# First batch of a fused two-layer graph attention kernel: the mask is shared between TensorE and VectorE, and the row sums leave GpSimd

## The chip, the cores and the metric

The kernel runs on one core of one Trainium2 chip. The metric is the device time of one execution in microseconds (us), the median of several runs. A core has five engines that work side by side: TensorE (PE in the profile, its weight loads PEld), VectorE (DVE), ScalarE (ACT), GpSimd (POOL), and SyncE (SP), which here only issues DMA transfers. Each engine takes its instructions strictly in the order in which the program wrote them.

## The reference, cut to what matters

There are 16 graphs (batches) of 1024 nodes with 256 features, and one 0/1 adjacency matrix per graph. Layer 0 is masked self-attention with 8 heads of width 32 followed by an MLP; layer 1 is a single-head graph attention. The change concerns the attention of layer 0:

```python
h = jnp.maximum(_layernorm(x), 0.0)
qkv = layer_norm(h, gamma1, beta1).reshape(b, n, 8, 32).transpose(0, 2, 1, 3)
scores = einsum('bhqd,bhkd->bhqk', qkv, qkv) / sqrt(32)
attn = softmax(where(adj > 0, scores, -inf), axis=-1)
out = einsum('bhqk,bhkd->bhqd', attn, qkv)
```

Queries, keys and values are the same matrix, the mask is symmetric and has the same value for all heads, and the softmax is taken without subtracting a maximum: the kernel computes exp(scale * (score + mask)), the weighted sum of values, and apart from it the row sum (the denominator).

## The kernel before, in words

One Python program writes out all 16 batches as straight-line code. Several generators ("streams") are merged by a place on a common axis, on which batch b's attention runs from b to b+1: attention (`stream_a`), the MLP and layer 1 of the batch (`stream_b`, which starts near b+0.98, so it runs beside the attention of batch b+1), the load and normalisation of the next batch (`stream_c`, `prologue`), and the load, conversion and transposition of the next masks (`stream_m`, `turn_masks`). `defer(us, f)` puts an operation off until a virtual clock has passed, and the order that comes out is the order of each engine's queue; dependencies add no engine order beyond that, since the last lines pin it. Because of these places the attention of batch 0 has no MLP beside it: only the setup of folded weights (`setup`), the second half of its own masks, and the prologue and first masks of batch 1.

The attention is cut into 32 units per batch: 2 query halves (`qh`, 512 queries) by 2 head groups (`g`, 4 heads) by 8 key tiles (`kt`, 128 keys). A unit in batch 0 is, in queue order:

- `scores`: two PSUM tiles `s` (`sc0` and `sc1`), 128 keys by 2 heads by 512 queries each, with one buffer each. TensorE first adds the mask with four matmuls of a full 128x128 fp8 identity against the mask (L874), then adds the products of keys and queries, four heads in four row groups of the array (L880, eight records because each fp32 matmul counts as two).
- ScalarE takes exp of `sc0` into `e` and later exp of `sc1` (L899).
- `weigh` of the unit before: value-weighted sums, four heads in four column quarters of the array (L912).
- `add_up` of a unit: `acc += e` for `sc0`'s half on VectorE and for `sc1`'s half on GpSimd (L931). In batches 1 to 15 the same sum is done by accumulating DMA transfers that GpSimd issues (L934).

From batch 1 on the mask isn't added by TensorE; VectorE adds it while it moves the scores from PSUM to SBUF (L896), and exp works in place. After the eight key tiles `total` multiplies `acc` by ones for the denominator (L835), `finish` transposes and divides (L852 to L859). The helper `matmul` (L567 to L570) splits a matmul into four column quarters of 32 while the flag `quarters` is set, which holds until the last attention is closed. `midp` is a pool of three 8 KB tiles (per partition) that the MLP's hidden layer and layer 1 use later and that holds the setup's `stage` at first; `ep` has five 4 KB tiles for `e`; `lp1` has six 2 KB tiles that layer 1 uses.

Of the kernel before, what the change touches and what calls it, by code (L numbers as in the profile page):

```python
# [9 lines left out]
F32 = mybir.dt.float32  # L10
# [6 lines left out]
P = 128  # L17
# [476 lines left out]
def fast_path(  # L494
# [28 lines left out]
    nc = tc.nc  # L523
    B, N, D = x.shape
    DFF = W1.shape[1]
    H, HD = 8, D // 8
    GH = 4
    NG = H // GH
    NT = N // P
    DC = D // P  # L530
    FC = DFF // P
    QW = 512
# [15 lines left out]
    midp = pool("midp", 3)  # L548
    ep = pool("ep", 5)
    accp = pool("accp", 2)  # L550
    lp1 = pool("lp1", 6)
# [6 lines left out]
    def ps_tile(shape, name, dtype=F32):  # L558
        return psm.tile(shape, dtype, tag="ps", name=name)
# [5 lines left out]
    def matmul(out, lhsT, rhs, start=True, stop=True):  # L565
        if not quarters[0]:
            nc.tensor.matmul(out, lhsT, rhs, start=start, stop=stop)  # L567
            return
        for c in range(0, P, HD):
            nc.tensor.matmul(out[c : c + HD], lhsT[:, c : c + HD], rhs, start=start, stop=stop)  # L570
# [30 lines left out]
    ones = const.tile([P, HD], F32, name="ones")  # L601
# [47 lines left out]


    def setup():
        stage = midp.tile([P, 4, DC, D], F32, tag="mid", name="stage")
        wl, wa, wT, wb = (stage[:, i] for i in range(4))
        weights_to_load.extend([(wl, W), (wa, a_12)])
        for t, src in weights_to_load:
            nc.scalar.dma_start(t, src.rearrange("(c p) n -> p c n", p=P))
        yield

        for oc in range(DC):
            pt = ps_tile([P, DC, P], f"p_wT_{oc}")  # L660
            for ic in range(DC):
                nc.tensor.transpose(pt[:, ic, :], wl[:, ic, oc * P : (oc + 1) * P], ident)
            nc.scalar.copy(wT[:, oc, :], pt.rearrange("p c q -> p (c q)"))
        clock[0] += 0.5
        yield

        def product(dst, lhs, rhs, n, name):

            for oc in range(DC):
                pp = ps_tile([P, n], f"p_{name}_{oc}")  # L670
                for kc in range(DC):
                    matmul(
                        pp,
                        lhs[:, kc, oc * P : (oc + 1) * P],
                        rhs[:, kc, :n],
                        start=(kc == 0),
                        stop=(kc == DC - 1),
                    )
                nc.scalar.copy(dst[:, oc, :], pp)

        product(wb, wa, wT, D, "wb")
        clock[0] += 1.7
        yield
        product(wm, wT, wb, D, "wm")
        product(w_a2.unsqueeze(2), wT, a2c.unsqueeze(2), 1, "w_a2")
        product(wo2[:, :, D : D + 1], wT, a1c.unsqueeze(2), 1, "w_a1")
        nc.gpsimd.memset(wo2[:, :, D + 1 : D + 2], 0.0)
        clock[0] += 2.0
        yield
# [22 lines left out]
    clock = [0.0]  # L712
    deferred = []

    def defer(us, f):
        deferred.append((clock[0] + us, len(deferred), f))

        return clock[0] + us
# [101 lines left out]
    def make_turns():  # L820
        room = 3 - open_sums[0] - bool(summed) if open_sums[0] else 100
        while turns and turns[0][0] <= room:
            n, f = turns.pop(0)
            room -= n
            f()
# [2 lines left out]

    scored, weighed, summed, totalled = [], [], [], []

    def total(b, qh, g, os, acc):

        den = ps_tile([P, QW], f"den_{b}_{g}_{qh}")
        for j in range(GH):
            nc.tensor.matmul(  # L835
                den[j * HD : (j + 1) * HD, :], ones, acc[j // 2][:, j % 2, :], start=True, stop=True
            )
        ds = tmpp.tile([P, QW], F32, tag="w2", bufs=3, name=f"ds_{b}_{g}_{qh}")
        nc.scalar.copy(ds, den)
        totalled.append((b, qh, g, ds, os))  # L840
# [20 lines left out]
    def attention(b, st):  # L861
        va, kT = st["va"], st["kT"]


        def scores(qh, g, kt):
            qs = slice(qh * QW, (qh + 1) * QW)
            sc = [
                psc.tile([P, 2, QW], F32, tag=f"sc{i}", name=f"s_{b}_{g}_{qh}_{kt}_{i}") for i in range(2)
            ]

            by_pe = b == 0
            if by_pe:
                for j in range(GH):
                    nc.tensor.matmul(  # L874
                        sc[j // 2][:, j % 2, :], ident8, st[qh][:, kt // 2, :, kt % 2], start=True, stop=False
                    )
                clock[0] += 0.9
            for j in range(GH):
                r = slice(j * HD, (j + 1) * HD)
                nc.tensor.matmul(  # L880
                    sc[j // 2][:, j % 2, :],
                    kT[r, g, kt * P : (kt + 1) * P],
                    kT[r, g, qs],
                    start=not by_pe,
                    stop=True,
                )
            mb = st[qh][:, kt // 2, :, kt % 2].unsqueeze(1).to_broadcast([P, 2, QW])
            es = []
            for i in range(2):
                if kt == 0:  # L890
                    e = accp.tile([P, 2, QW], F32, tag=f"acc{i}", name=f"acc_{b}_{g}_{qh}_{i}")
                else:
                    e = ep.tile([P, 2, QW], F32, tag="e", name=f"e_{b}_{g}_{qh}_{kt}_{i}")
                masked = sc[i]
                if not by_pe:
                    nc.vector.tensor_tensor(e, masked, mb, op=ALU.add)  # L896
                    masked = e
                es.append(e)
                weights = lambda e=e, masked=masked: nc.scalar.activation(e, masked, AF.Exp, scale=SCALE)  # L899
                if i == 0:  # L900
                    weights()
            return es, weights

        acc = {}


        def weigh(qh, g, kt, es):
            if kt == 0:
                acc[g, qh] = pso.tile([P, QW], F32, tag="o", name=f"o_{b}_{g}_{qh}")
            o = acc[g, qh]  # L910
            for j in range(GH):
                nc.tensor.matmul(  # L912
                    o[j * HD : (j + 1) * HD, :],
                    va[:, kt, (g * GH + j) * HD : (g * GH + j + 1) * HD],
                    es[j // 2][:, j % 2, :],
                    start=(kt == 0),
                    stop=(kt == NT - 1),
                )
            if kt == NT - 1:
                c = tmpp.tile([P, QW], F32, tag="w2", bufs=3, name=f"os_{b}_{g}_{qh}")  # L920
                nc.vector.tensor_copy(c, o)
                weighed.append((b, qh, g, c, sums[g, qh]))

        sums = {}


        def add_up(qh, g, kt, es):
            if b == 0:

                for e, a, engine in zip(es, sums[g, qh], (nc.vector, nc.gpsimd)):  # L930
                    engine.tensor_add(a, a, e)  # L931
                return
            for e, a in zip(es, sums[g, qh]):
                nc.gpsimd.dma_start(a, e, accum_op=ALU.add)  # L934

        units = [(qh, g, kt) for qh in range(NQH) for g in range(NG) for kt in range(NT)]
        for u in units:
            make_turns()
            es, rest_of_weights = scores(*u)
            go_on()  # L940
            rest_of_weights()
            qh, g, kt = u
            if kt == 0:
                sums[g, qh] = es
            else:
                defer(1.5, lambda u=u, es=es: add_up(*u, es))
            scored.append((weigh, (*u, es)))
            yield

    def go_on():  # L950
        was_weighed, was_summed, was_totalled = weighed[:], summed[:], totalled[:]
        for l in (weighed, summed, totalled):
            l.clear()
        if scored:
            f, args = scored.pop()
            f(*args)
        summed.extend(was_weighed)
        for args in was_summed:
            total(*args)
        for args in was_totalled:  # L960
            turns.append((2, lambda args=args: finish(*args)))
        clock[0] += 2.0
# [320 lines left out]
    def stream_a():  # L1283
        for b in range(B):
            yield from spread(attention(b, states[b]), 32, b, b + 1)
        yield from spread(close_attention(), 4, B, B + 0.05)
# [40 lines left out]
    def stream_s():  # L1327
        yield -0.3
        for i, _ in enumerate(setup()):
            yield 0.25 + 0.05 * i  # L1330
# [3 lines left out]
    while any(p is not None for p in places):  # L1334
        i = min((p, i) for i, p in enumerate(places) if p is not None)[1]
# [101 lines left out]
```

## Time and profile before

| what | value |
|---|---|
| device time, median of 3 | 3644.68 us (3642.08 to 3649.2) |
| span of the profiled execution | 3643.5 us, granted TensorE clock 0.991 |
| VectorE busy over the span | 2749.6 us (75%) |
| ScalarE busy | 1859.1 us (51%) |
| GpSimd busy | 1483.6 us (41%) |
| first mask matmul of batch 0 | at 41.47 us |
| last score matmuls of batch 0 | at 175.67 us |
| first MLP matmul | at 182.55 us |

The first batch's attention thus takes 141 us of 3643.5 us; what precedes it is the load of the first inputs and masks. Durations are of one instruction, busy times are unions of them, and "idle before" is how long the engine had stood still before the instruction, with what released it. An instruction that is stretched by another engine counts as busy for its whole length, so a long mean must be compared with the length of the same instruction elsewhere.

### The profile page before, as it was taken

How to read it: one execution, taken by the hardware profiler on the slowest of the kernel's cores; microseconds unless marked ns; L12 is line 12 of the kernel's file. 1: busy time of each engine (PE TensorE's matmuls, PEld its weight loads, DVE VectorE, ACT ScalarE, POOL GpSimd, SP SyncE). 2: the span in 40 equal slices, each digit the busy share in tenths (PEclk: the TensorE clock that was granted, in tenths of full speed). 3: DMA queues.
4: the chain of work that ended last, by engine and by line, in shares of the span. 5: the costliest groups of instructions: out<-in, count | busy, mean ns of one | idle time of the engine just before them, and what ended most of it. 6: DMA issues, size and time to landing. Idle time of an engine off the chain costs nothing.

```text
span 3643.5 us, 106813 instructions
## 1 busy us (share of the span) xinstructions
PE 3501.1 (96%) x46334; PEld 1697.8 (47%) x46334; DVE 2749.6 (75%) x5165; ACT 1859.1 (51%) x2183; POOL 1483.6 (41%) x1712
## 2 busy tenths in 40 slices
PE   5899999999999999999999999999999999999998
PEld 1244444444444444444444444444444444444477
DVE  3878878787786978768787787877868777786744
ACT  3555555555555555545555555555555555555522
POOL 4844434343443434434444343433434344343220
PEclk9999999999999999999999999999999999999999
DMA  3278988989889988888988889888988989899720
GB/s 100 67 145 169 181 164 178 191 166 177 170 177 176 175 173 169 175 157 179 189 166 168 164 174 189 170 178 164 182 168 176 169 166 181 162 180 180 148 49 13
DMA packets 278978, 585.19 MB, mean 161 GB/s; under 512 B 94562, under 2 KB 129764, under 8 KB 278500
## 3 DMA queue, kind: packets, MB, share of 16 engines
q0 software_dynamic: 120960, 440.46, 65.9%
q1 hardware_dynamic: 152580, 134.27, 14.3%
q8 instruction: 366, 6.00, 0.7%
q10 hardware_dynamic: 4960, 3.55, 0.4%
q14 instruction: 112, 0.92, 0.1%
HBM read 104.21 MB, written 16.78 MB: 33 GB/s over the span
## 4 chain that ended last, share of the span: by engine, by line
PE 75%; DMA 10%; DVE 7%; issue 4%; ACT 2%; POOL 2%; DVEq 0%; POOLq 0%; SPq 0%; ACTq 0%
PE s L880 13%; PE o L912 11%; PE pa L570 10%; PE ph L570 10%; PE lg L570 9%; DMA acc<-e 9%; PE po L570 7%; PE pf L570 2%; DVE e L896 2%; PE pg L570 2%; PE puT L570 2%; PE den L835 1%; ACT e L899 1%; DVE e L1153 1%; PE pa L567 1%
## 5 line engine op out<-in xcount | busy, mean ns | idle before, releaser
L899 ACT ACTIVATE e<-e 128x1024 f32<-128x1024 f32 x840 | 884.8, 1057 | 1018.8 <-DVE e L896 763.5
L934 POOL DMA_DIRECT2D acc<-e x840 | 740.3, 893 | 1553.4 <-DMA acc<-e 680.3
L896 DVE TENSOR_TENSOR e<-s,mk 128x1024 f32<-128x1024 f32 x840 | 988.5, 1217 | 170.3 <-PE s L880 96.1
L880 PE MATMUL s<-kT 32*128 32x512 f32 x4096 | 617.1, 649 | 3.9 <-DVE e L896 3.9
L912 PE MATMUL o<-e,va 128*32 128x512 f32 x3584 | 487.3, 614 | 1.6 <-ACT e L899 1.6
L570 PE MATMUL ph<-yT,w 128*32 128x256 f32 x7808 | 450.2, 381 | 4.7 <-DVE yT L1033 4.7
L570 PE MATMUL pa<-gw,e 128*32 128x258 f32 x7552 | 449.1, 382 | 0.0
L570 PE MATMUL lg<-fT,uT 128*32 128x256 f32 x7680 | 445.1, 379 | 0.0
L570 PE MATMUL po<-w,hid 128*32 128x256 f32 x7680 | 441.8, 381 | 0.0
L570 PEld LDWEIGHTS ph<-yT,w 128*32 128x32 f32 x7808 | 254.9, 110 | 220.1 <-issue 54.0
L570 PEld LDWEIGHTS po<-w,hid 128*32 128x32 f32 x7680 | 251.4, 111 | 211.6 <-issue 66.2
L570 PEld LDWEIGHTS pa<-gw,e 128*32 128x32 f32 x7552 | 251.3, 111 | 210.8 <-issue 63.1
L570 PEld LDWEIGHTS lg<-fT,uT 128*32 128x32 f32 x7680 | 250.3, 110 | 209.0 <-issue 39.6
L1153 DVE SCALAR_TENSOR_TENSOR e<-lg,gw,mk 128x256 f32<-128x256 f32 x512 | 223.0, 476 | 65.5 <-PE lg L570 57.2
L1056 DVE TENSOR_TENSOR hid<-ph,b1c 128x512 f32<-128x512 f32 x256 | 175.1, 687 | 125.6 <-PE ph L570 112.2
L1159 ACT ACTIVATE e<-e,shift 128x512 f32<-128x512 f32 x256 | 183.0, 716 | 139.6 <-DVE e L1158 114.8
L880 PEld LDWEIGHTS s<-kT 32*128 32x128 f32 x4096 | 170.8, 185 | 174.7 <-issue 106.8
L912 PEld LDWEIGHTS o<-e,va 128*32 128x32 f32 x3584 | 71.7, 108 | 348.3 <-issue 202.7
L1158 DVE SCALAR_TENSOR_TENSOR e<-e 128x512 f32<-128x512 f32 x256 | 198.6, 776 | 8.8
L899 ACT ACTIVATE acc<-acc 128x1024 f32<-128x1024 f32 x120 | 126.9, 1058 | 143.5 <-DVE acc L896 139.1
L769 POOL TENSOR_TENSOR nrm<-nrm,g 128x256 f32<-128x256 f32 x128 | 118.9, 929 | 85.0 <-DVE nrm L706 85.0
L896 DVE TENSOR_TENSOR acc<-s,mk 128x1024 f32<-128x1024 f32 x120 | 141.1, 1217 | 14.3 <-PE s L880 14.3
(136 smaller groups left out, 3939.9 us busy)
## 6 DMA issues: line engine op xcount, KB each, us to landing
acc<-e POOLq DMA_DIRECT2D x840, 512.0 KB, 5.9
adj<-in_adj_dram SPq DMA_DIRECT2D x256, 256.0 KB, 5.0
h<-in_x_dram SPq DMA_DIRECT2D x64, 256.0 KB, 7.1
xb<-in_x_dram SPq DMA_DIRECT2D x128, 128.0 KB, 5.3
out_dram<-z SPq DMA_DIRECT2D x128, 128.0 KB, 3.1
w<-in_L_gnn_W_dram ACTq DMA_DIRECT2D x2, 1024.0 KB, 10.3
mk<-mq SPq DMA_TRANSPOSE x128, 6.2
wo<-in_L_gnn_W_dram ACTq DMA_DIRECT2D x2, 256.0 KB, 3.9
```

What stands on the lines that cost most here:

```text
L567: nc.tensor.matmul(out, lhsT, rhs, start=start, stop=stop)
L570: nc.tensor.matmul(out[c : c + HD], lhsT[:, c : c + HD], rhs, start=start, stop=stop)
L769: nc.gpsimd.tensor_mul(nrm, nrm, g1)
L880: nc.tensor.matmul(sc[j // 2][:, j % 2, :], kT[r, g, kt * P : (kt + 1) * P], kT[r, g, qs], start=not by_pe, stop=True,)
L896: nc.vector.tensor_tensor(e, masked, mb, op=ALU.add)
L899: weights = lambda e=e, masked=masked: nc.scalar.activation(e, masked, AF.Exp, scale=SCALE)
L912: nc.tensor.matmul(o[j * HD : (j + 1) * HD, :], va[:, kt, (g * GH + j) * HD : (g * GH + j + 1) * HD], es[j // 2][:, j % 2, :], start=(kt = ...
L934: nc.gpsimd.dma_start(a, e, accum_op=ALU.add)
L1056: nc.vector.tensor_tensor(hid[:, f0 : f0 + 2, :], ph, b1c[:, f0 : f0 + 2].unsqueeze(2).to_broadcast([P, 2, CW]), op=ALU.add,)
L1153: nc.vector.scalar_tensor_tensor(e[:, j, :], lg[:, j, :], gw[:, kt, D : D + 1], st[c // 2][:, kt // 2, qs, kt % 2], op0=ALU.add, op1=ALU.add,)
L1158: nc.vector.scalar_tensor_tensor(e, e, ALPHA, e, op0=ALU.mult, op1=ALU.max)
L1159: ready = defer(2.5, lambda: nc.scalar.activation(e, e, AF.Exp, bias=shift))
```

## The change

Only batch 0 is touched, apart from the place of the setup's staging tiles.

- Mask: TensorE adds it only for heads 0 and 1 (`sc0`), through `matmul`, so in column quarters. For heads 2 and 3 VectorE adds it as in the later batches, `e = sc1 + mask`, and exp works in place. The virtual clock counts 0.45 us for it in place of 0.9.
- Row sums: GpSimd adds nothing. Even key tiles go into `acc` by accumulating DMA as in the later batches. Odd key tiles go into tiles `odd` of the pool `midp`; VectorE adds the former odd tile to the present one, half by half, deferred by 1.0 and 3.5 us after `weigh`.
- `total` multiplies both `acc` and the last `odd` by ones and sums in PSUM.
- `stage` moves from one 8 KB tile of `midp` to four 2 KB tiles of `lp1`, which leaves all three `midp` tiles for `odd`.

The purpose is to take half of the mask matmuls from TensorE and all of the 128x1024 additions from GpSimd.

```diff
--- before.py
+++ after.py
@@ -649,8 +649,7 @@
 
 
     def setup():
-        stage = midp.tile([P, 4, DC, D], F32, tag="mid", name="stage")
-        wl, wa, wT, wb = (stage[:, i] for i in range(4))
+        wl, wa, wT, wb = (lp1.tile([P, DC, D], F32, tag="e1", name=f"stage_{i}") for i in range(4))
         weights_to_load.extend([(wl, W), (wa, a_12)])
         for t, src in weights_to_load:
             nc.scalar.dma_start(t, src.rearrange("(c p) n -> p c n", p=P))
@@ -828,13 +827,18 @@
 
     scored, weighed, summed, totalled = [], [], [], []
 
-    def total(b, qh, g, os, acc):
+    def total(b, qh, g, os, accs):
 
         den = ps_tile([P, QW], f"den_{b}_{g}_{qh}")
         for j in range(GH):
-            nc.tensor.matmul(
-                den[j * HD : (j + 1) * HD, :], ones, acc[j // 2][:, j % 2, :], start=True, stop=True
-            )
+            for acc in accs:
+                nc.tensor.matmul(
+                    den[j * HD : (j + 1) * HD, :],
+                    ones,
+                    acc[j // 2][:, j % 2, :],
+                    start=acc is accs[0],
+                    stop=acc is accs[-1],
+                )
         ds = tmpp.tile([P, QW], F32, tag="w2", bufs=3, name=f"ds_{b}_{g}_{qh}")
         nc.scalar.copy(ds, den)
         totalled.append((b, qh, g, ds, os))
@@ -868,31 +872,36 @@
                 psc.tile([P, 2, QW], F32, tag=f"sc{i}", name=f"s_{b}_{g}_{qh}_{kt}_{i}") for i in range(2)
             ]
 
-            by_pe = b == 0
+            by_pe = 2 if b == 0 else 0
             if by_pe:
-                for j in range(GH):
-                    nc.tensor.matmul(
+                for j in range(by_pe):
+                    matmul(
                         sc[j // 2][:, j % 2, :], ident8, st[qh][:, kt // 2, :, kt % 2], start=True, stop=False
                     )
-                clock[0] += 0.9
+                clock[0] += 0.45
             for j in range(GH):
                 r = slice(j * HD, (j + 1) * HD)
                 nc.tensor.matmul(
                     sc[j // 2][:, j % 2, :],
                     kT[r, g, kt * P : (kt + 1) * P],
                     kT[r, g, qs],
-                    start=not by_pe,
+                    start=j >= by_pe,
                     stop=True,
                 )
             mb = st[qh][:, kt // 2, :, kt % 2].unsqueeze(1).to_broadcast([P, 2, QW])
             es = []
+            if b == 0 and kt % 2:
+
+                odd = midp.tile([P, 2, 2, QW], F32, tag="mid", name=f"odd_{g}_{qh}_{kt}")
             for i in range(2):
-                if kt == 0:
+                if b == 0 and kt % 2:
+                    e = odd[:, i]
+                elif kt == 0:
                     e = accp.tile([P, 2, QW], F32, tag=f"acc{i}", name=f"acc_{b}_{g}_{qh}_{i}")
                 else:
                     e = ep.tile([P, 2, QW], F32, tag="e", name=f"e_{b}_{g}_{qh}_{kt}_{i}")
                 masked = sc[i]
-                if not by_pe:
+                if 2 * i >= by_pe:
                     nc.vector.tensor_tensor(e, masked, mb, op=ALU.add)
                     masked = e
                 es.append(e)
@@ -916,19 +925,22 @@
                     start=(kt == 0),
                     stop=(kt == NT - 1),
                 )
+            if b == 0 and kt % 2:
+
+                if kt > 1:
+                    for n, (e, w) in enumerate(zip(es, odds[g, qh])):
+                        defer(1.0 + 2.5 * n, lambda e=e, w=w: nc.vector.tensor_add(e, e, w))
+                odds[g, qh] = es
             if kt == NT - 1:
                 c = tmpp.tile([P, QW], F32, tag="w2", bufs=3, name=f"os_{b}_{g}_{qh}")
                 nc.vector.tensor_copy(c, o)
-                weighed.append((b, qh, g, c, sums[g, qh]))
-
-        sums = {}
+                weighed.append((b, qh, g, c, [s[g, qh] for s in (sums, odds) if s]))
+
+        sums, odds = {}, {}
 
 
         def add_up(qh, g, kt, es):
-            if b == 0:
-
-                for e, a, engine in zip(es, sums[g, qh], (nc.vector, nc.gpsimd)):
-                    engine.tensor_add(a, a, e)
+            if b == 0 and kt % 2:
                 return
             for e, a in zip(es, sums[g, qh]):
                 nc.gpsimd.dma_start(a, e, accum_op=ALU.add)
```

## Prediction

> **What bounds the kernel now.** I read the page's busy times first, then the busy times by stretch, to see how the first batch differs from a later one.
>
> ```profile
> PE 3501.1 (96%) x46334; PEld 1697.8 (47%) x46334; DVE 2749.6 (75%) x5165; ACT 1859.1 (51%) x2183; POOL 1483.6 (41%) x1712
> 41.00:180.00 139.00, 119.11 (x840) 37.11 (x840) 89.95 (x119) 73.47 (x91) 100.78 (x64) 0.99 0.22 58
> 300.00:420.00 120.00, 117.94 (x1668) 57.39 (x1664) 102.41 (x190) 66.50 (x87) 52.97 (x63) 1.00 0.84 166
> ```
>
> TensorE is the bound over the whole: 96% busy, and 117.9 of 120 us in a later stretch. The columns of the last two lines are the length, then PE, PEld, DVE, ACT, POOL busy, clock, DMA share, GB/s. In the first batch's attention (41 to 180 us) TensorE has 20 us of gaps. Since TensorE is the bound from there on, time saved before 182 us moves the end one to one. Next the chain of waits inside that stretch, where nothing but attention runs:
>
> ```profile
> 62.19 0.59 PE s L874 x2
> 62.78 1.14 PE s L880 x8
> 63.92 0.02 issue
> 63.94 0.04 ACT e L899
> 63.98 0.88 issue
> 64.86 1.03 ACT e L899
> 65.89 0.04 issue
> 65.93 0.59 PE s L874 x2
> ```
>
> This is one unit, 62.19 to 65.93, 3.74 us: mask of sc1, scores (their weighing follows and lies beside the exps), exp of sc0 (the "issue" of 0.88), exp of sc1, and only then the next mask of sc1. TensorE and ScalarE alternate in a ring because each s tile has one buffer. Then the groups of VectorE and GpSimd in 41 to 180 us, and the same mask conversion after 300 us:
>
> ```profile
> L931 POOL TENSOR_TENSOR acc<-acc,e 128x1024 f32<-128x1024 f32 x27 | 69.7, 2580 | 25.5 <-ACT e L899 25.1
> L591 DVE TENSOR_SCALAR mq<-adj 128x512 fp8e5<-128x512 int32 x16 | 19.6, 1247 | 5.4 <-DMA adj<-in_adj_dram 5.4
> L754 DVE SCALAR_TENSOR_TENSOR nm<-mv_a,rs_a 128x2 f32<-128x2 f32 x4 | 5.5, 1364 | 0.6 <-POOL rs_a L702 0.6
> ...
> L591 DVE TENSOR_SCALAR mq<-adj x224: 411/419/1276, 350.2 to 3347.1; 128x512 fp8e5<-128x512 int32 x112
> ...
> 177.19 4.86 DVE L706 TENSOR_SCALAR y<-h,mv_c,rs_c 128x256 f32<-128x256 f32 x2
> 182.55 3.19 PE L570 MATMUL ph<-yT,w 128*32 128x256 f32 x32 [4.75 <-DVE yT L1033]
> ```
>
> A conversion takes 1247 ns in the mean beside GpSimd's additions and 419 ns later. The last two lines (timeline) show what it costs: two normalisations of 0.36 us last 4.86 us, and TensorE stands idle for 4.75 us before the first MLP matmul.
>
> **What the Trainium skill says.** "SBUF — State Buffer", Who interferes with whom: VectorE and GpSimd share one port pair as an exclusive lock; a VectorE instruction with at most one SBUF input outside the two-port modes doesn't contend, one with two SBUF inputs contends with a GpSimd instruction that reads SBUF. The stretched rows agree. The new mask addition reads PSUM and one SBUF operand, so it should keep L896's 1217 ns. "TensorEngine Tiling (Array Packing)", Key Properties: tiles work in parallel, and changing the tiling mode drains the array. The trace agrees on the parallel part: eight quarter records of the denominator, 592 ns each, end within 1.04 us. "GPSIMD Engine Reference", Engine selection: a two-input elementwise operation is about 2 times slower there than on VectorE; here 2416 against 1224 ns (medians).
>
> **The change part by part.** A clean unit after the change: mask of sc0 (0.59 us, as two full matmuls now; see below), scores 1.08, step to ScalarE 0.09, exp of sc0 1.03, step back 0.08, and the next mask of sc0 can start: 2.87 us, 0.87 less. Beside this ring: VectorE's mask addition 1.22 and exp of sc1 1.03 end 2.4 us after the scores, before the next unit needs either; ScalarE has 2.06 us of exps per unit; TensorE 0.59 + 1.08 + 1.00 = 2.67 us.
>
> The mask in quarters isn't in the trace. Eight quarters at the overlap of the fp32 quarters, one pass of 512 columns, give what two full fp8 matmuls take, 0.59 us. This is the near bound. If the quarters didn't overlap, eight issues at the 0.21 us that full ones are apart would be 1.7 + 0.16 = 1.87 us. I take 0.59, since the fp32 quarter matmuls of this trace overlap.
>
> VectorE loses 26 additions (36.2 us) and gains 32 mask additions (39 us) and 24 odd additions of 1.22 (29 us), but no longer stands in GpSimd's lock: conversions fall from 1.25 to 0.43 us (13 us), nm, ve and y together from 20 to 4 us. GpSimd keeps 24 transfers' issue at 0.86 us (21 us), where it had 70 us of additions. A transfer lands 5.9 us after issue; the next into the same acc comes two units later, 5.7 us or more, and the denominator is asked for three to four units after the last, 10 us or more: hidden. The last denominator has 16 records in place of 8, 0.85 us more.
>
> VectorE's queue now has a mask addition in every unit, and behind it the odd additions, conversions and statistics. A conversion waits for its adjacency rows, which are fetched only when the former conversion has freed the buffer: some 3.9 us by the trace. Where two conversions have only one unit between them (units 9 and 25) VectorE stands still, about 1.5 and 0.8 us, and the next mask addition with it, so scores of sc1 too. I price each interval between two units at the longer of the ring plus TensorE's extras (denominator 1.87, weight products 1.73 and 2.6, transpositions 0.6 to 1.0) and VectorE's queue in the order that the program writes:
>
> - To the scores of unit 7: cold start as before, unit 1 ends at 48.1 us (before 49.0), then six rings of 2.87 and one transposition: 65.7 us. Before: 71.3. Gain 5.6.
> - Units 7 to 31: VectorE's pieces are 82 us in sum, TensorE's ring with extras 85 us; the sum of the longer ones, interval by interval, is 99 us (it runs from 2.9 in intervals with one odd addition to 4.0 to 5.2 where statistics, conversion or the denominator stand, and 6.2 at the second weight product). Before: 176.8 - 71.3 = 105.5. The queues smooth a little, one unit deep; I take 97. Gain 8.5.
> - The hand-over to the MLP: the normalised rows stand before unit 31's mask addition in VectorE's queue, with no lock, so the MLP's first matmul follows the last weighing. Gain 4.75, less 0.85 for the denominator: 3.9.
>
> Sum: 5.6 + 8.5 + 3.9 = 18.0 us. Moving the stage tiles to lp1 costs nothing, since layer 1 uses that pool first after 180 us. Three odd tiles are enough: an odd tile is free two odd units later, after its sum. From batch 1 on the queues are the same instructions in the same order but for a few lines at the border. 3644.7 - 18.0 = 3626.7, say 3627 us.
>
> **The rivals.** (a) The intervals overlap better, to the bound of the busier engine (85 us): gain 18 + 12 = 30, 3615 us. For it speaks that neither engine is full; against it, that in-order queues with single PSUM buffers let neither work ahead. (b) VectorE becomes the ring: new locks (24 odd additions with two SBUF inputs against about 35 GpSimd operations of 0.7 us) and waits for adjacency rows push every interval beyond unit 7 up by 0.4 us, so 10 us are given back: 3637 us. For it speaks VectorE's load in the last group (30 us of pieces in eight units); against it, that most GpSimd work is gone. (c) The quarter masks don't overlap: the ring becomes 2.87 + 1.28 = 4.15 us, which over 31 units with TensorE's 17 us of extras is about 145 us from 41.5 us to the scores of unit 31, against 135 before, with the hand-over's 3.9 still gained: slower by about 6 us, 3651 us. For it: no such instruction in the trace. Against: the fp32 quarters.
>
> **How the numbers follow.** Forecast (main case, 3620 to 3634) 0.62, (a) 0.13, (b) 0.17, (c) 0.08. The range 3614 to 3641 takes in (a) and (b) and leaves (c) out. Within 0.2% is 3637.4 to 3652: half of (b) and a fraction of (c), 0.12; slower most of (c), 0.06; faster 0.82.
>
> **What would show it.** Right: in clean units of the first group the chain repeats mask, scores, exp of sc0 every 2.9 us; conversions at about 0.43 us; mask additions at 1.22; the quarter mask group 0.6 us per unit; the first MLP matmul near 164 us, with no long idle before it. Wrong: quarter masks that follow one another in time; VectorE's mask addition waiting behind "DMA adj" or a stretched odd addition for several us; a denominator that waits for "DMA acc"; or later batches that take up the gain in longer gaps.

## The result and the profile after

The changed kernel takes 3621.66 us (median of four runs, 3611.66 to 3630.88), the kernel before 3644.11 us: a ratio of 0.9936, 95% interval 0.9907 to 0.9964. In a second series on one chip, six runs against eleven, the ratio was 0.9953, 0.9937 to 0.9970. The change makes the kernel faster by about half a per cent, and the forecast of 3627 us with its range of 3614 to 3641 us holds the time.

The same views as before, of the changed kernel: the page's busy times and the busy times by stretch.

```profile
PE 3496.7 (96%) x46494; PEld 1695.6 (47%) x46494; DVE 2751.8 (76%) x5193; ACT 1863.1 (51%) x2183; POOL 1428.1 (39%) x1708
41.00:180.00 139.00, 128.24 (x1202) 42.57 (x1196) 108.50 (x166) 87.76 (x102) 59.17 (x69) 0.99 0.75 155
300.00:420.00 120.00, 118.06 (x1696) 57.54 (x1692) 101.97 (x191) 65.29 (x78) 53.43 (x63) 1.00 0.95 183
```

From 41 to 180 us TensorE is busy for 128 us in place of 119, VectorE for 108 in place of 90, and GpSimd for 59 in place of 101; the last 20 us of this stretch are already MLP here. The later stretch is as it was. The chain of waits in the clean units of batch 0:

```profile
53.45 0.61 PE s L570 x8
54.06 1.08 PE s L884 x8
55.14 0.02 issue
55.17 1.03 ACT e L908
56.20 0.04 issue
56.24 0.61 PE s L570 x8
```

One ring is now mask of sc0, scores, exp of sc0: 53.45 to 56.24 is 2.79 us in place of 3.74. The exp of sc1 has left the chain. VectorE's groups from 41 to 180 us, and the first MLP matmul in the timeline:

```profile
L932 DVE TENSOR_TENSOR odd<-odd,odd 128x1024 f32<-128x1024 f32 x24 | 29.7, 1236 | 0.3 <-PE o L921 0.3
L905 DVE TENSOR_TENSOR odd<-s,mk 128x1024 f32<-128x1024 f32 x16 | 19.6, 1222 | 9.7 <-PE s L884 9.7
L591 DVE TENSOR_SCALAR mq<-adj 128x512 fp8e5<-128x512 int32 x16 | 6.5, 438 | 5.9 <-DMA adj<-in_adj_dram 5.9
L753 DVE SCALAR_TENSOR_TENSOR nm<-mv_a,rs_a 128x2 f32<-128x2 f32 x4 | 1.7, 422 | 0.0
...
159.69 1.91 PE L570 MATMUL ph<-yT,w 128*32 128x256 f32 x32
```

The conversion is back at 438 ns from 1247, nm at 422 from 1364; the new mask addition takes 1.22 us and the new addition of odd tiles 1.24. The first MLP matmul comes at 159.69 us, before at 182.55: 22.9 us gained. The wait of 4.75 us in front of it is gone. The medians differ by 22.5 us; the two profiled executions differ by only 14.8 (3643.5 against 3628.7). What is missing there fits the granted clock, as one stretch far behind the change shows, first of the kernel before:

```profile
600.00:700.00 100.00, 100.00 (x1447) 48.63 (x1443) 75.12 (x126) 51.48 (x53) 39.49 (x48) 1.00 0.89 177
```

and the same stretch of the changed kernel:

```profile
600.00:700.00 100.00, 94.44 (x1286) 44.41 (x1280) 64.31 (x116) 48.62 (x47) 36.35 (x44) 0.95 0.98 170
```

A clock of 0.95 over 100 us costs 5 us of TensorE's work, and the next 100 us are at 0.98 against 1.00. Summed over the 36 stretches of 100 us, the clock was short by 40 us' worth in this execution and by 31 in the profile of before. A second profile of the changed kernel was short by 29, and its span was 3618.5 us, 25.0 under that of before. The runs of one kernel differ by up to 19 us, so for the mechanism the start of the first MLP matmul is the better measure: it was 159.69 and 159.33 us in the two profiles of the changed kernel.

### The profile page after: what moved, and what is told of

Same layout as the page of the kernel before. It is cut to its first block, busy times and chain, and to the rows that moved or that the text cites. A ratio compares the mean times of both kernels' runs of the same rounds, so it can differ in the third digit from the quotient of the medians.

```text
span 3628.7 us, 107138 instructions
## 1 busy us (share of the span) xinstructions
PE 3496.7 (96%) x46494; PEld 1695.6 (47%) x46494; DVE 2751.8 (76%) x5193; ACT 1863.1 (51%) x2183; POOL 1428.1 (39%) x1708
## 4 chain that ended last, share of the span: by engine, by line
PE 83%; DVE 7%; DMA 6%; issue 2%; ACT 1%; POOL 1%; ACTq 0%; DVEq 0%; POOLq 0%; SPq 0%
PE s L884 14%; PE o L921 12%; PE ph L570 12%; PE pa L570 11%; PE lg L570 9%; PE po L570 9%; DMA acc<-e 5%; PE pf L570 2%; DVE e L905 2%; PE puT L570 2%; PE pg L570 2%; PE den L835 2%; PE ptk L776 1%; PE pty L1041 1%; PE pa L567 1%
## 5 line engine op out<-in xcount | busy, mean ns | idle before, releaser
L908 ACT ACTIVATE e<-e 128x1024 f32<-128x1024 f32 x852 | 897.6, 1057 | 1023.8 <-DVE e L905 764.8
L946 POOL DMA_DIRECT2D acc<-e x864 | 761.3, 892 | 1604.3 <-DMA acc<-e 674.0
L905 DVE TENSOR_TENSOR e<-s,mk 128x1024 f32<-128x1024 f32 x852 | 1003.2, 1218 | 162.1 <-PE s L884 98.7
L921 PE MATMUL o<-e,va 128*32 128x512 f32 x3456 | 471.3, 615 | 2.1 <-ACT e L908 2.1
```

The lines of the kernel that those rows point to most:

```text
L921: nc.tensor.matmul(o[j * HD : (j + 1) * HD, :], va[:, kt, (g * GH + j) * HD : (g * GH + j + 1) * HD], es[j // 2][:, j % 2, :], start=(kt = ...
```

## The experiments

The theory was that two limits held batch 0: the ring through both exps, and GpSimd's additions, which are slow themselves and stretch VectorE. The rival was that one of them alone makes the time. In all diffs the changed kernel is the starting point; "..." stands for lines left out. Where no ratio is given, the variant ran once, and its device time says little beside a spread of 19 us: what counts is its first MLP matmul. A group is eight units with one accumulator, so unit 7, counted from 0, ends the first of the four groups.

**The mask alone, with the former row sums.**

```diff
-            if b == 0 and kt % 2:
+            if False:
 
                 odd = midp.tile([P, 2, 2, QW], F32, tag="mid", name=f"odd_{g}_{qh}_{kt}")
...
 def add_up(qh, g, kt, es):
-            if b == 0 and kt % 2:
+            if b == 0:
+                for e, a, engine in zip(es, sums[g, qh], (nc.vector, nc.gpsimd)):
+                    engine.tensor_add(a, a, e)
                 return
```

> The mask is split as in the change, the row sums stay as before (VectorE and GpSimd). First MLP matmul: before 182.55 us, changed kernel 159.69. Theory A (two causes: the ring of mask and exps, and GpSimd's additions with their lock): the first eight units run at 2.8 us as in the changed kernel, so the scores of unit 7 end near 64 us, but GpSimd needs 2.4 us for its addition in each unit and stretches VectorE, so the later groups fall back and the first MLP matmul comes at 172 to 178 us. Theory B (the ring alone): first MLP matmul at 159 to 164 us.

The first MLP matmul came at 188.73 us, 6 us later than before the change: over the whole stage the mask alone loses. In the first group it gains, as the theory said: the scores of unit 7 ended at 65.05 us (theory 64, before 71.34), and the denominator came at 76.72 in place of 84.35. At the second denominator the lead was 1.8 us, and at the third the run was 4.3 us behind (155.28 against 150.96). Both forecasts of the end were too early. The granted clock was 0.85 from 100 to 160 us, so the kernel ran once more.

> The split mask with the former row sums once more, because in its first run the granted clock was 0.91 in the first batch. If GpSimd's additions and their lock set the pace, the clock hardly matters: at a clock near 1.0 the first MLP matmul comes at 182 to 190 us, VectorE's additions keep a median near 2.2 us. If the low clock made the time: 165 to 175 us.

188.92 us, and the same low clock from 100 us on (0.74 from 120 to 140 us), so the second run doesn't take the clock away as a cause for the later groups. The first group had a clock of 1.00. The scores of its last unit, and its chain of waits in the second run:

```profile
63.25 1.88 PE L884 MATMUL s<-kT 32*128 32x512 f32 x8
...
56.11 0.14 DVE e L905
56.25 1.00 issue
57.25 1.37 DVE acc L945
58.62 0.81 issue
59.43 0.14 DVE e L905
59.57 1.00 issue
60.56 1.33 DVE acc L945
```

VectorE's row-sum addition in this run, and in the first group of the kernel before (min, median and max of its duration in ns):

```profile
L945 DVE TENSOR_TENSOR acc<-acc,e x26: 1207/2246/3193, 50.9 to 184.4; 128x1024 f32<-128x1024 f32 x26
...
L931 DVE TENSOR_TENSOR acc<-acc,e x6: 1224/1224/1226, 50.1 to 68.7; 128x1024 f32<-128x1024 f32 x6
```

VectorE's additions come every 3.3 us, not every 2.79: the mask addition of 1.22 and a row-sum addition whose median is 2246 ns. Its shortest took 1207 ns, and the same form takes 1236 ns in the changed kernel, where GpSimd adds nothing. Their number is much the same (28 in the batch here, 24 there), so it is their length that counts. Now VectorE stands in the ring, so each stretched addition delays the next mask. Before, no mask waited for it, and in that group it wasn't stretched. But 3.3 us is still less than the former 3.74, so the loss arises in the later groups, where statistics and conversions come to VectorE as well. The busy times there, with those of TensorE first and VectorE third:

```profile
80.00:189.00 109.00, 89.42 (x652) 27.47 (x656) 101.57 (x126) 50.38 (x62) 76.61 (x51) 0.85 0.22 61
```

VectorE is busy for 101.6 of 109 us, where before it was busy for 81.8 of 102.5 us up to the first MLP matmul. VectorE's mask addition took 1.21 to 1.23 us at every granted clock of TensorE in these runs, so this work would be there at a full clock too. By an estimate from it alone, 80 + 101.6, the stage can't end before about 182 us, far from the 159 to 164 us of the rival. Whether the last 7 us come from VectorE's waits or from the low clock isn't settled.

**The row sums alone, with the mask on TensorE for all heads.**

```diff
-            by_pe = 2 if b == 0 else 0
+            by_pe = 4 if b == 0 else 0
...
-                    matmul(
+                    nc.tensor.matmul(
...
-                clock[0] += 0.45
+                clock[0] += 0.9
```

> The row sums are as in the change, the mask is added by TensorE for all four heads as before. Theory A: the ring stays at 3.7 us in clean units, so the scores of unit 7 end near 71 us; without the lock the later units keep to about that pace and the hand-over's idle time is gone, first MLP matmul at 164 to 170 us. Theory B (the ring alone matters): 176 to 182 us.

171.89 us, with a clock of 1.00 throughout: 10.7 us gained, between the theory's 164 to 170 and the rival's 176 to 182, and nearer to the theory's. The timeline of TensorE in clean units:

```profile
61.26 0.59 PE L878 MATMUL s<-mk,ident 128*128 128x512 fp8e5 x2 [0.32 <-ACT e L908]
61.78 1.14 PE L884 MATMUL s<-kT 32*128 32x512 f32 x8
62.86 1.06 PE L921 MATMUL o<-e,va 128*32 128x512 f32 x8
64.03 0.59 PE L878 MATMUL s<-mk,ident 128*128 128x512 fp8e5 x2
64.95 0.59 PE L878 MATMUL s<-mk,ident 128*128 128x512 fp8e5 x2 [0.32 <-ACT odd L908]
65.47 1.14 PE L884 MATMUL s<-kT 32*128 32x512 f32 x8
```

Scores follow at 61.78 and 65.47, 3.69 us: the old ring, with the second mask waiting for the second exp. So the parts don't add up: the mask alone loses 6 us, the sums alone gain 10.7, both gain 22.9. Once GpSimd adds nothing, the split mask is worth 12.2 us (171.89 to 159.69). In these runs the shorter ring is of use to the end of the stage only there.

**Full matmuls in place of column quarters for the two masks.**

```diff
-                    matmul(
+                    nc.tensor.matmul(
                         sc[j // 2][:, j % 2, :], ident8, ...
```

> As the changed kernel, but the two mask matmuls of a unit use the full 128x128 array in place of column quarters. If quarters cost what full ones cost, and the ring hides what is left: first MLP matmul at 158.5 to 161 us. If the change of tiling mode counts: 0.1 to 0.2 us for each unit, so 163 to 166 us, with clean units at 2.9 to 3.0 us in place of 2.79.

159.67 us, against 159.69. A clean unit takes 2.77 us, from the chain of waits of this run:

```profile
53.39 0.59 PE s L878 x2
53.98 1.08 PE s L884 x8
55.06 0.02 issue
55.09 1.03 ACT e L908
56.12 0.04 issue
56.16 0.59 PE s L878 x2
```

Two full matmuls take 0.59 us and eight quarters 0.61: the quarters overlap, and save nothing in these units. A cost of one more change of tiling mode isn't visible here.

**VectorE adds the mask for all four heads.**

```diff
-            by_pe = 2 if b == 0 else 0
+            by_pe = 0
```

> As the changed kernel, but VectorE adds the mask for all four heads of batch 0, as in the later batches, and TensorE for none. VectorE's work per unit rises from about 3.1 to 4.3 us, so if VectorE is next in line behind the ring, the stage grows by 25 to 38 us: first MLP matmul at 185 to 198 us, later than before the change. If the ring or TensorE were still the limit: at most 165 us.

> The mask by VectorE alone with the new row sums once more, because its first run had a granted clock of 0.86 there. If VectorE's load sets the pace: first MLP matmul at 174 to 180 us at a clock near 1.0. If the clock made it: 160 to 167 us.

179.16 and 179.26 us, 19.5 us later than the changed kernel and earlier than the first forecast's 185. The granted clock was 0.78 and 0.77 from 100 to 160 us in the two runs, with TensorE busy for 17 to 19 of every 20 us there, so the clock can have a share. The busy times of the first run behind 80 us:

```profile
80.00:179.00 99.00, 86.83 (x516) 24.95 (x508) 89.13 (x143) 53.06 (x63) 38.51 (x47) 0.83 0.69 141
```

VectorE's 89 us of work alone put the first MLP matmul at 169 us or later, by the same estimate as above: at least about half of the 19.5 us is VectorE's load. How the rest divides between its waits and the clock isn't settled by these runs. What was measured is that half and half came before either whole: 171.9 (all TensorE), 159.7 (half), 179.2 (all VectorE), each with the new row sums.

**All row sums by DMA.** The odd tiles fall away; every key tile but the first goes into the accumulator by a transfer.

```diff
...
 def add_up(qh, g, kt, es):
-            if b == 0 and kt % 2:
-                return
             for e, a in zip(es, sums[g, qh]):
                 nc.gpsimd.dma_start(a, e, accum_op=ALU.add)
```

> As the changed kernel, but all seven row-sum additions of a group go by accumulating DMA, none through odd tiles. If one transfer into an accumulator must land before the next starts, some 5 to 6 us each against a unit of 2.8 to 4 us, the groups become a chain of transfers: first MLP matmul at 185 to 210 us. If transfers overlap: VectorE loses 29 us of additions and the first MLP matmul comes at 140 to 150 us.

221.50 us, later than the forecast of a chain of transfers, and a device time of 3689.45 us. The sum by line at the head of this run's chain of waits, 41 to 220 us:

```profile
by line: DMA acc<-e 65.8%; issue 9.1%; PE s L884 4.5%; DVE e L905 4.1%; ACT e L908 3.0%; POOL nrm L768 2.5%; PE s L570 2.2%; POOL va L769 2.1%; POOL acc L944 2.0%; PE o L921 1.6%; PE den L835 1.5%; POOL rs_b L701 0.7%; PE p_wT L661 0.6%; PE
```

Two thirds of the stage are transfers that follow one another, 6.0 us each in the median. The odd tiles are what keeps this chain at three transfers per accumulator, in place of seven.

**The waits that are left.** In the changed kernel VectorE still waits 5.9 us for adjacency rows. The chain of waits shows the worst of it (device time in us, length, what):

```profile
142.64 0.76 DVE mq L591 x2
143.40 0.12 DVE nrm L705
143.52 6.60 DMA adj<-in_adj_dram
150.14 0.43 DVE mq L591
...
151.76 1.23 DVE odd L905
152.99 0.04 issue
153.03 1.22 PE s L884 x4
```

The mask addition at 151.76 stands behind that conversion and 1.2 us of statistics, and TensorE's scores stand behind the addition. Two edits aimed at such waits, one by one and together. The first spreads the loads and conversions of the next masks over twice the length, the second puts off an activation of batch 1's prologue:

```diff
-                yield from spread(turn_masks(b, qh, states[b]), 5, b + 0.5 * qh - 0.27, b + 0.5 * qh - 0.07)
+                lead = 0.47 if (b, qh) in ((0, 1), (1, 0)) else 0.27
+                yield from spread(turn_masks(b, qh, states[b]), 5, b + 0.5 * qh - lead, b + 0.5 * qh - 0.07)
```

```diff
-                nc.scalar.activation(h[:, t, :], ..., AF.Relu, ...)
+                rect = lambda t=t, j=j: nc.scalar.activation(h[:, t, :], ..., AF.Relu, ...)
+                defer(2.2, rect) if b == 1 else rect()
```

> As the changed kernel, but the loads and conversions of the masks for batch 0's second query half and batch 1's first are spread over twice the length, starting earlier, so that a conversion comes 2.6 units after its fetch in place of 1.3. If VectorE's waits for adjacency rows (5.9 us in the changed kernel) stand on the path: they fall under 1.5 us and the first MLP matmul comes at 153 to 157 us. If VectorE's load bounds these units anyway: 158 to 161 us.

> As the changed kernel, but in batch 1's prologue the rectifying activation on ScalarE is put off by 2.2 us of the virtual clock, so that exps queue ahead of it and don't wait for VectorE's nm. In the changed kernel the chain shows three places where nm and the activation hold the next exp (near 93, 115 and 127 us), with 1.0, 2.1 and 0.8 us of TensorE idle. If these are on the path: first MLP matmul at 155.5 to 157.5 us. If VectorE's queue is late there anyway: 158.5 to 160.5 us.

> The changed kernel with both the early mask loads and the late rectifying activation. If the two waits are separate: first MLP matmul at 152 to 155 us, and a device time 5 to 8 us under the changed kernel's. If one covers the other: 155 to 157 us and 2 to 4 us.

The early masks brought the first MLP matmul to 156.68 us and VectorE's waits for rows to 1.7 us, as the theory said. The late activation did nothing (159.47). This is the forecast's second case; that VectorE is late there anyway was not shown apart from it. Both together were at 163.53 us, against both forecasts: the first denominator waited for a transfer into the accumulator that took 13.2 us from issue to landing (66.75 to 79.92 us). The early masks alone were then timed in a series.

> The changed kernel with the early mask loads, timed. First MLP matmul at 156 to 158 us as in its first run; if that carries to the end, a median 3 us under the changed kernel's, ratio to the kernel before 0.992 to 0.996, which can't be told from the changed kernel's.

> The changed kernel again, for a comparison on the same chip in the same rounds. If the time gained in the first batch (22.9 us to the first MLP matmul) carries to the end: ratio 0.9937 (22.9 of 3640), within 0.002. If later batches give it back: ratio 0.997 or more.

The same kernel that had 156.68 us now had 162.21. Its chain of waits:

```profile
65.22 1.06 ACT odd L908
66.28 0.54 ACT stage L662 x2
66.82 0.24 issue
67.06 12.99 DMA acc<-e
80.05 0.04 issue
80.10 0.42 PE den L835
```

It is the same transfer as with both edits: 13 us from issue to landing, where the median is 6. The denominator stood behind it, and the next units behind that. In the first run of the early masks the longest landing was 10.1 us, and no denominator waited in this group. So two of the three runs with early masks had the long landing, while no such transfer took over 9.4 us in the changed kernel's two profiles or with the late activation alone. With the early masks a mask transpose is issued at 64.6 us, just before this transfer, and the next loads and transpose at 70 to 74 us; in the changed kernel there is neither between 60 and 70 us. That the transposes hold up the transfer is possible, and not shown.

Times: 3618.86 us with both edits (ratio to before 0.9939, 0.9921 to 0.9958), 3623.18 with the early masks (0.9938, 0.9919 to 0.9957), 3623.72 for the changed kernel (0.9953, 0.9937 to 0.9970). No variant can be told from the change itself. The changed kernel's 0.9953 lies within what was expected if the 22.9 us carry to the end (0.9937 within 0.002); that later batches give back a part isn't excluded by this interval. Its six runs had a mean granted clock of 0.991 and the eleven of before 0.993. A straight line through these seventeen runs, with one slope for both kernels, gives 3.0 us for each 0.001 of clock, and 22.8 us between the kernels at the same clock (standard error 2.0). This estimate speaks for the whole gain; it assumes that the lower clock isn't the change's own doing, which was not tested.

## Why the prediction was right

- **The time and the milestones.** That the median fell into the range is a weak test beside a spread of 19 us. The stronger one is the first MLP matmul: 159.69 us where 164 was forecast, with every part of the gain present and each somewhat larger.
- **The ring.** Forecast 2.87 us, measured 2.79. The steps between engines (0.09 and 0.08) were mis-sized: they measure 0.02 and 0.04, since the matmuls' 1.08 already reaches nearly to the exp's start. With a cold start that came 1.8 us earlier than forecast, the scores of unit 7 ended at 63.52 us (forecast 65.7, before 71.34): a gain of 7.8 us in place of 5.6.
- **Units 7 to 31.** Forecast 97 us, measured 95.4 (to 158.88 us), between the bound of the busier engine (85) and the interval-by-interval sum (99), close to the latter. Gain 10.1 in place of 8.5. Rival (a) overrated how much the queues smooth. The closeness is in part luck: VectorE's waits for rows came to 5.9 us where 2.3 were priced, so other intervals were priced too high. The shorter ring is at most 1.9 us of this (24 times 0.08).
- **The hand-over.** 0.8 us from the last scores to the MLP in place of 5.7: a gain of 4.9, forecast 3.9, because the longer last denominator comes only after the MLP has begun, at 173.60 us. The sum is 22.8 against the forecast's 18.0.
- **The quarter masks.** Forecast 0.59 us, measured 0.61; rival (c) falls by that line, and the run with full matmuls confirms that it doesn't matter which.
- **VectorE's lock.** The conversions, nm and the rest shrank as forecast. "SBUF — State Buffer", Who interferes with whom, which says that a VectorE instruction with two SBUF inputs contends with a GpSimd instruction that reads SBUF, agrees with the run of the mask alone: 2246 ns in the median with GpSimd's additions, 1236 ns in the mean without. It also agrees with the mask addition, which has one SBUF input and stayed at 1.22 us in every run. The forecast said that the stretched rows agree with the rule as it gave it; for the conversion that doesn't follow, since it has one SBUF input and yet fell from 1247 to 438 ns. Which mode it ran in, no run shows. What the forecast didn't see is that the two parts depend on each other.
- **The waits.** Two of the forecast's signs of being wrong did show, but small. Rival (b)'s waits for rows are 5.9 us in five waits, where the forecast named 1.5 and 0.8 us at units 9 and 25; the worst was between units 28 and 29, where rows took over 6 us to land. And one denominator waited for a transfer into acc: at 134.41 us it took 3.51 us in place of 1.75, since its second half could start only at 136.00.

## What to carry to other kernels

A share of work moved to an engine can lose if that engine is held by another: here the same mask split lost 6 us beside GpSimd's additions and gained 12 when they were gone, so two changes may have to be made together. A variant that loses over the whole stage may still win in its first part, so compare milestones, not only the end. For these in-order queues with single buffers, the sum over intervals of the slower engine (99 us) came nearer to the measured 95.4 than the larger of the engines' total loads (85). When a small gain is to be found in runs that spread by half a per cent, measure the start of the next stage in the profile, and look at the granted clock before explaining what follows.

## What the runs showed of the hardware beyond that

- The granted clock depends on the kernel and repeats. From 100 to 160 us it was 0.85 in both runs of the mask alone, 0.78 and 0.77 in both runs with the mask on VectorE, and 0.80 with all sums by DMA. It was 0.94 to 1.00 in the other variants. These averages hide changes within a few us: with the mask on VectorE it was 1.00 from 93 to 96 us and 0.52 from 96 to 102. The longest wait of TensorE in that run was 2.0 us from 80 to 180 us. How long TensorE was busy doesn't separate the kernels: 51, 53 and 48 of the 60 us in the three low ones, 51 in the kernel before, at 1.00, and 54 in the changed one, at 0.97. No run here separates the cause.
- The landing of one 512 KB accumulating transfer between SBUF tiles ranges from 4.5 to 9.4 us in the two profiles of the changed kernel, and to 13 us in two of three runs with the early masks; the same kernel's stage moved by 5.5 us with it.
